# Four steps of a graph network moved to GpSimd, quarter tiles in its last layer, and a new planned order

## The chip, the cores and the metric

The kernel runs on one core of a Trainium2 chip. The metric is the device time of one execution in microseconds (us). Before the change it is 2740.81 us, the median of 3 runs (2739.89 to 2741.58).

## The reference

A stack of four graph layers on 16 independent graphs of 1024 nodes with 256 features; each layer takes `relu(layernorm(x))` and adds its result to x.

```python
# layer 0
h = h_in @ W_msg                                  # messages
msg = einsum('bij,biu->bju', adj, h) / deg        # sum over neighbours
x += relu(h_in @ W_upd + msg + bias)
# layers 1 and 2: attention with 4 heads of 64 (slope 0.01 and 0.2)
e = leaky_relu(e_src[i] + e_dst[j], slope)        # where adj, else -1e9
x += epilogue(softmax(e) @ h)   # 1: bias, relu, + h, layernorm per head; 2: elu
# layer 3: the same with one head of 256, slope 0.2, no epilogue
```

adj holds zeros and ones, is symmetric and has ones on its diagonal; some 3% of its entries are ones. All is float32.

## The kernel before

`tile_factored` does the work; `tile_general` is a second way that runs only if a check at the end (sums of adj, sizes of the exponents, denominators) is not met. With s and d the source and target terms, exp(leaky_relu(s+d)) is exp(slope s) exp(d) times the larger of exp((1-slope) s) and exp(-(1-slope) d), and the first factor drops out of the softmax, so that one VectorE instruction gives 128 x 1024 weights: `masked` (L1077) takes the maximum of a broadcast row r, which holds exp((1-slope) s) of the 1024 sources, with a per-partition scalar tt = exp(-(1-slope) d), and multiplies by the 0/1 mask. These tiles are called masks or weights here; they are the stationary side of the products. exp(d) is multiplied into the other side (`weigh`, L1242, for layers 1 and 2; a ScalarE scaling, L1407, for layer 3).

Per graph:
- layer 0: `norm_t` (norm and transposition: statistics on VectorE L922 and L929, a power on GpSimd L934 and L935, normalisation on ScalarE L954, transposition on PE L967). Four pairs of projections (L984) of the messages; each pair is split into a high part in the PE's rounded float32 format (ScalarE L1112) and a low part: PE subtracts the high one in PSUM with a product by minus identity (L1119), ScalarE copies the rest (L1129). Eight gathers (L1143, L1146) sum both over the neighbours. Each gather's result is scaled by the inverse degree (GpSimd L1157 and L1158, ScalarE L1164). For each pair of node blocks, PE adds the bias as a product of two rows (L1173) to the update projection (L1182); VectorE adds both (L1194) and adds the relu to x (L1201).
- `mask_block` loads adj, squares it on ScalarE into bytes and transposes it by DMA into the mask.
- layers 1 and 2, `heads`: norm, eight projections (L984, copied by ScalarE at L1003), `terms` (L1009): exp of the source terms on ScalarE (L1024), transposed on PE (L1034), copied (L1038), stored to DRAM by SP (L1042) and broadcast back as r, one row per head (L1067); VectorE's reductions for the range check (L1050 to L1052); two exponentials of d (L1057, L1058); `weigh`. Then for each of four heads eight masks of 128 x 1024 and eight products (L1266, 16 matmuls each), and an epilogue: division (L1285, L1286), layer 1's bias, relu, norm (L1310 to L1369), layer 2's elu (ScalarE L1381, L1382, VectorE L1388). Results of heads 0 to 2 go to x by an accumulating DMA from GpSimd's queue (L1216), that of head 3 by VectorE (L1227).
- layer 3: eight masks of 128 x 256 for each of four pairs of target blocks (L1083 with 256 columns), products of two matmuls (L1420), division and sum (L1434, L1445), store.

The order of all engines is written out by a planner (`Plan`, L72). Each step is given with `do`: engine, an assumed cost, reads, writes and a due time: the PE time of the steps of its graph before it, plus `b * SHIFT` (L1472), plus a constant per stage and engine (`RANK`). `emit` then repeatedly takes, of all steps that are ready, the one that can start first, with the smallest due time among equals, and gives out its instructions in that sequence. So several graphs are interleaved; each engine works its queue strictly in that order. `BUFS` (L52) says how many buffers stand behind each name: six mask buffers `p`, four PSUM banks `mm`, two of `hn`. `gates` lets a graph begin once the second before it has reached layer 3.

In the planned order of the steady part, PE's transposition of the source terms of layer 1 (L1034) of a graph is followed by 12 matmuls of layer 3 of the second graph before it (L1420), and then by that layer's first product. VectorE's order there: last scaling, last layer-2 epilogue of the graph before, norm statistics for that graph's layer 3, and then the first masks of layer 1.

Of the kernel before, what the change touches and what calls it, by code (L numbers as in the profile page):

```python
# [26 lines left out]
SHIFT = 38.75  # L27

ENGINES = ("pe", "dve", "act", "pool", "sp")
RANK = {  # L30
    "load": (-255, -45, -146, -223, -161),
    "setup": (147, 44, -129, 45, 72),
    "norm0": (132, -159, -111, 18, -3),
    "split0": (-94, 119, -51, -165, -111),
    "mask": (77, 143, 41, 193, 218),
    "gather0": (241, -7, 71, 23, 10),
    "norm1": (-60, -62, -162, -146, -99),
    "project1": (20, 26, -5, 26, -6),
    "weights1": (-164, 7, -45, 57, -13),
    "heads1": (-192, -212, -213, -62, -111),  # L40
    "last1": (-26, -102, 9, -196, -80),
    "norm2": (-206, -157, 81, 6, -21),
    "project2": (79, -60, -360, 87, -40),
    "weights2": (94, -3, 153, -153, 12),
    "heads2": (-112, -33, -288, -105, -59),
    "last2": (-21, -230, -230, -36, -82),
    "norm3": (-477, -373, -518, -355, -261),
    "project3": (148, 162, -14, -78, 0),
    "weights3": (170, 143, 167, 44, 87),
    "last3": (43, -259, -75, -14, -59),  # L50
# [4 lines left out]
    "mv": 4, "st": 2, "rstd": 4, "shift": 4, "tt": 3, "es": 2, "dg": 2, "rden": 2, "sth": 1, "mh": 2, "rsh": 2,  # L55
    "acc": 2, "mm": 4,
    "f_w0": 1, "f_w1": 1, "f_w2": 1, "f_w3": 1, "f_bias0": 1, "f_rows1": 1,
# [14 lines left out]
class Plan:  # L72
# [8 lines left out]
    def __init__(self):  # L81
        self.ops, self.pos, self.gate, self.stage = [], 0.0, None, None

    def do(self, eng, cost, fn, r=(), w=(), lag=0.0, slack=0.0, kind="f", dma=0.0):
# [25 lines left out]
        self.ops.append((eng, cost, lag, fn, deps, bufs, self.pos + slack + RANK[self.stage][ENGINES.index(eng)], kind, dma))  # L110
# [3 lines left out]
    def emit(self):  # L114
# [7 lines left out]
        kept, moved = "f", 0.0  # L122
# [6 lines left out]
        while ready:  # L129
            best = None  # L130
            for k in ready:
                eng, cost, lag, fn, deps, bufs, prio, kind, dma = self.ops[k]
# [18 lines left out]
                if at is not None and (best is None or (at, prio, k) < best):  # L151
                    best = (at, prio, k)
# [446 lines left out]
def tile_factored(  # L599
# [75 lines left out]
    def kept(name, shape, dtype=F32):  # L675

        t = const.tile(shape, dtype, name=name)
        return Buf(name, lambda: t)


    w0 = kept("f_w0", [P, KC, 2 * D])
    w1c = kept("f_w1", [P, KC, WC])
# [868 lines left out]
```

## Time and profile before

| | us |
|---|---|
| median of 3 runs | 2740.81 |
| the profiled execution's own time | 2741.27 |
| its span in the profile | 2739.4 |
| PE busy | 2547.4 |
| VectorE (DVE) busy | 2357.3 |
| ScalarE (ACT) busy | 1143.5 |
| GpSimd (POOL) busy | 878.0 |

The mean granted PE clock is 0.972 of full. Two queues carry nearly all of the 293.58 MB that DMA moves. The costliest groups are the masks (L1083, 1536 instructions, 1473.3 us on VectorE) and the products of layers 1 and 2 (L1266, 1064.6 us on PE).

A row of groups reads: line, engine, operation, output<-inputs, shape, x count | busy us, mean ns of one | idle time of the engine just before them, and what ended most of it. A row of the timeline: start, duration, engine, line, operation, and in brackets the idle time before it with what ended it. PE records two matmuls for each float32 matmul of the text.

### The profile page before, as it was taken

Reading aid. Unit: us, or ns where it says so; the run is one execution under the profiler, and the core shown is the slowest. Engines: PE = TensorE matmul, PEld = TensorE weight load, DVE = VectorE, ACT = ScalarE, POOL = GpSimd, SP = SyncE. Lnnn points to the kernel's source line nnn. Section 1 sums busy time; section 2 is a strip of 40 time slices with the busy share of each in tenths; the row PEclk is TensorE's granted clock in tenths of the full one; section 3 lists DMA queues with packets and bytes.
Section 4 is the critical chain, followed back from the end, with each engine's and each line's share of the span. In section 5 each row is a group of like instructions: output and inputs, shape, how many; then the busy total and the mean of one; then the engine's idle time right before and its main releaser. Section 6 shows DMA issues by size and latency. Waiting matters only on the chain. (4 is left out here: it accounts for less than half of the span.)

```text
span 2739.4 us, 92386 instructions
## 1 busy us (share of the span) xinstructions
PE 2547.4 (93%) x40667; PEld 2285.7 (83%) x40667; DVE 2357.3 (86%) x4790; ACT 1143.5 (42%) x2753; POOL 878.0 (32%) x907
## 2 busy tenths in 40 slices
PE   7867999999999999999999999999999999999786
PEld 6767798888888888889888889888888988888775
DVE  2699689898988989899898989989898898989884
ACT  4431625344353444525344452534435353453222
POOL 3332234324252332424224251422425133241210
PEclk9989999999999999999999999999999999999998
DMA  8724547356472745547255563735546263562121
GB/s 194 171 44 84 113 87 165 82 128 117 99 143 53 159 91 129 105 91 163 60 144 97 118 125 71 163 75 133 112 107 134 63 158 81 130 118 66 33 52 29
DMA packets 397318, 293.58 MB, mean 107 GB/s; under 512 B 179301, under 2 KB 345706, under 8 KB 396906
## 3 DMA queue, kind: packets, MB, share of 16 engines
q0 software_dynamic: 232992, 92.29, 24.8%
q1 hardware_dynamic: 160752, 193.05, 24.4%
q8 instruction: 321, 5.26, 0.8%
q10 hardware_dynamic: 3162, 2.24, 0.3%
q14 instruction: 91, 0.75, 0.1%
HBM read 228.21 MB, written 17.37 MB: 90 GB/s over the span
## 5 line engine op out<-in xcount | busy, mean ns | idle before, releaser
L1083 DVE SCALAR_TENSOR_TENSOR p<-r,tt,mask 128x1024 f32<-128x1024 f32 (+1 forms) x1536 | 1473.3, 1010 | 109.2 <-PE acc L1266 40.8
L1266 PE MATMUL acc<-wide,p 128*64 128x65 f32 x32768 | 1064.6, 227 | 135.7 <-DVE p L1083 129.3
L1266 PEld LDWEIGHTS acc<-wide,p 128*64 128x64 f32 x32768 | 1017.2, 141 | 204.0 <-issue 99.0
L984 PE MATMUL mm<-f_w,ht 128*128 128x264 f32 (+2 forms) x2048 | 477.0, 387 | 1.4 <-ACT ht L973 1.3
L1420 PE MATMUL acc<-wide,p 128*128 128x257 f32 x2048 | 462.2, 382 | 10.1 <-DVE p L1083 9.9
L1420 PEld LDWEIGHTS acc<-wide,p 128*128 128x128 f32 x2048 | 386.1, 191 | 68.1 <-issue 11.1
L984 PEld LDWEIGHTS mm<-f_w,ht 128*128 128x128 f32 x2048 | 384.6, 192 | 61.2 <-ACT ht L973 3.0
L954 ACT ACTIVATE hn<-x,shift,rstd 128x256 f32<-128x256 f32 x512 | 269.1, 591 | 257.5 <-DVE shift L941 157.1
L1356 ACT ACTIVATE t<-t,mh,rsh 128x64 f32<-128x64 f32 x512 | 176.7, 428 | 198.2 <-DVE mh L1346 174.3
L1143 PE MATMUL mm<-wide,adjr 128*128 128x258 f32 x1024 | 254.5, 289 | 0.0
L1146 PE MATMUL mm<-wide,adjr 128*128 128x256 f32 x1024 | 247.9, 282 | 0.0
L1003 ACT COPY wide<-mm 128x264 f32<-128x264 f32 (+1 forms) x384 | 141.3, 378 | 218.7 <-PE mm L984 216.5
L1216 POOL DMA_DIRECT2D x<-y x48 | 76.6, 1596 | 447.4 <-DVE y L1388 435.8
L934 POOL TENSOR_SCALAR rstd<-mv 128x4 f32<-128x4 f32 x128 | 60.7, 474 | 434.6 <-DVE mv L929 402.3
L1143 PEld LDWEIGHTS mm<-wide,adjr 128*128 128x128 f32 x1024 | 195.9, 191 | 1.7
L1146 PEld LDWEIGHTS mm<-wide,adjr 128*128 128x128 f32 x1024 | 194.2, 190 | 1.5
L922 DVE BATCH_NORM_STATS2 st<-x 128x6 f32<-128x256 f32 x512 | 183.2, 412 | 8.4 <-DMA x<-in_x_dram 5.6
L967 PE MATMUL mm<-f_ident,hn 128*128 128x128 f32 x1024 | 168.0, 300 | 20.2 <-ACT hn L954 17.2
L973 ACT COPY ht<-mm 128x512 f32<-128x512 f32 x256 | 137.8, 580 | 104.9 <-PE mm L967 103.9
L1157 POOL TENSOR_SCALAR dg<-f_deg 128x1 f32<-128x1 f32 x128 | 61.0, 476 | 359.7 <-ACT f_deg L1154 357.4
L967 PEld LDWEIGHTS mm<-f_ident,hn 128*128 128x128 f32 x1024 | 125.2, 151 | 50.4 <-ACT hn L954 35.5
L935 POOL TENSOR_TENSOR rstd<-rstd,f_mhalf 128x4 f32<-128x4 f32 x128 | 162.2, 1268 | 10.7
(103 smaller groups left out, 2179.3 us busy)
## 6 DMA issues: line engine op xcount, KB each, us to landing
r<-rd SPq DMA_DIRECT2D x144, 512.0 KB, 3.9
adjr<-in_adj_dram POOLq DMA_DIRECT2D x128, 512.0 KB, 4.7
nat<-in_adj_dram SPq DMA_DIRECT2D x128, 512.0 KB, 6.6
out_dram<-o SPq DMA_DIRECT2D x64, 256.0 KB, 2.8
x<-in_x_dram SPq DMA_DIRECT2D x31, 512.0 KB, 5.1
x<-t POOLq DMA_DIRECT2D x48, 256.0 KB, 5.5
x<-y POOLq DMA_DIRECT2D x48, 256.0 KB, 4.5
mask<-sq SPq DMA_TRANSPOSE x128, 4.7
```

What stands on the lines that cost most here:

```text
L922: lambda st=st, ib=ib, k=k: nc.vector.bn_stats(st.t[:, k, :], xs.t[:, ib, :]),
L935: nc.gpsimd.tensor_tensor(rstd.t, rstd.t, mhalf[:, :nh], op=ALU.pow)
L954: nc.scalar.activation(hn.t[:, k, :], xs.t[:, hf * nh + q, :], AF.Relu, bias=shift.t[:, q : q + 1], scale=rstd.t[:, q : q + 1],)
L967: nc.tensor.transpose(pt.t[:, k, c, :], hn.t[:, k, c * P : (c + 1) * P], ident)
L984: nc.tensor.matmul(out, ht.t[:, c, ib * P : (ib + 1) * P], w.t[:, c, lo:hi], start=(c == 0 and k == 0), stop=(c == KC - 1), skip_group_che ...
L1003: lambda ib=ib, ps=ps: nc.scalar.copy(wh.t[:, ib, :cols], ps.t[:, :cols]),
L1083: lambda: nc.vector.scalar_tensor_tensor(w.t[:, : hi - lo], r.t[:, lo:hi], tt.t[:, jb, h : h + 1], mask.t[:, jb, lo:hi], op0=ALU.max, op1= ...
L1143: nc.tensor.matmul(ps.t[:, : D + 2], a.t[:, ib, :], hi.t[:, ib, : D + 2], start=(ib == 0), stop=False)
L1146: nc.tensor.matmul(ps.t[:, :D], a.t[:, ib, :], lo.t[:, ib, :D], start=False, stop=(ib == NB - 1))
L1266: nc.tensor.matmul(ps.t[c : c + 64, g, q * E1 : (q + 1) * E1], p.t[:, i2 * 64 : (i2 + 1) * 64], xw.t[:, jb, h * E1 : (h + 1) * E1], start= ...
L1356: nc.scalar.activation(t.t[:, ib, :], t.t[:, ib, :], AF.Identity, bias=mb.t[:, 3, ib : ib + 1], scale=rs.t[:, ib : ib + 1],)
L1420: nc.tensor.matmul(ps.t[:, q, : D + 1], w.t[:, q * P : (q + 1) * P], wh.t[:, jb, : D + 1], start=(jb == 0), stop=(jb == NB - 1),)
```

## The change

- Low part of the messages: ScalarE copies the projection from PSUM to SBUF (into one of the two `hn` buffers) and GpSimd subtracts the high part (64 instructions of 128 x 512). PE's product by minus identity is gone.
- Layer 0's bias is loaded once to all partitions and added by GpSimd to the scaled sums (64 of 128 x 512); PE's bias product is gone, and so is the preparation of its two rows.
- Range check: GpSimd adds exponentials up over all layers and graphs (two additions of at most 64 columns in each of 48 layers), and one comparison at the end takes the largest sums; VectorE's three reductions per layer are gone.
- Scaling by exp(d) (`weigh`) goes from VectorE to GpSimd, 64 of 128 x 1024, with the small copies of layer 1.
- Layer 3: four masks of 256 columns share one `p` buffer.
- The planner: other costs, ranks and start offsets per graph (`START`), a tolerance within which a step of smaller due time goes first (`HOLD`), masks kept in one sequence per graph (`row`), and masks preferred when few are in stock (`LOW`, `FIRST`). The source terms' copy gets a buffer of its own (`r4`).

In the order that results, the transposition of layer 1's source terms is, for graphs 2 to 14, followed on PE at once by the first product of that layer. On VectorE the sequence at that place is the last layer-2 epilogue, the norm statistics of layer 3, and the first mask. At the start, graph 0 passes through layers 1 and 2 before graph 1's first product of layer 1.

```diff
-SHIFT = 38.75
+SHIFT = 101.5
+
+LOW, FIRST = 1, 28
 
 ENGINES = ("pe", "dve", "act", "pool", "sp")
+HOLD = (0.0, 0.05, 0.6, 0.0, 0.0)
+
+START = (232, 385, 200, 255, 176, 24, -46, -173, -79, -112, -264, -136, -283, -240, -391, -668)
...
-    "weights1": (-164, 7, -45, 57, -13),
+    "weights1": (-173, -73, -356, -76, 0),
...
-    "mv": 4, "st": 2, "rstd": 4, "shift": 4, "tt": 3, "es": 2, "dg": 2, "rden": 2, "sth": 1, "mh": 2, "rsh": 2,
+    "mv": 4, "st": 2, "rstd": 4, "shift": 4, "et": 3, "r4": 1, "dg": 2, "rden": 2, "sth": 1, "mh": 2, "rsh": 2,
...
+        if row is not None:
+            if row in self.rows:
+                deps.add(self.rows[row])
+            self.rows[row] = k
...
+                if stock > 0 and store < LOW:
+                    prio -= FIRST
...
+            until = at + HOLD[ENGINES.index(self.ops[k][0])]
+            for a, p, q in could:
+                if self.ops[q][0] == self.ops[k][0] and a <= until and p < prio:
+                    at, prio, k = a, p, q
+            eng, cost, lag, fn, deps, bufs, _, kind, dma, stock = self.ops[k]
+            store += stock
...
+        fetch(b0, "in", lambda t: t, bias0.rearrange("(o d) -> o d", o=1).to_broadcast([P, D]))
...
+        def raise_t():
+            nc.scalar.activation(et.t[:, 1], ed().rearrange("p n h -> p h n"), AF.Exp, scale=-(1.0 - slope))
+            nc.scalar.activation(ed(), ed(), AF.Exp)
+
+        do("act", 0.5, raise_t, w=[(et, 1), wh])
+
         def bounds():
-            es = wh.t[:, :, scol : scol + nh]
-            nc.vector.tensor_reduce(mx[:, k : k + 1], ed(), AX.XY, ALU.max)
-            nc.vector.tensor_reduce(mx[:, k + 1 : k + 2], ed(), AX.XY, ALU.min, negate=True)
-            nc.vector.tensor_reduce(mx[:, k + 2 : k + 3], es, AX.XY, ALU.max)
-
-        do("dve", 0.4, bounds, r=[wh])
-
-        def raise_t():
-            nc.scalar.activation(tt.t, ed(), AF.Exp, scale=-(1.0 - slope))
-            nc.scalar.activation(ed(), ed(), AF.Exp)
-
-        do("act", 0.5, raise_t, w=[tt, wh])
+            so_far = top
+            nc.gpsimd.tensor_tensor(
+                so_far[:, :2, :m], so_far[:, :2, :m], et.t.rearrange("p s h n -> p s (h n)"), op=ALU.add
+            )
+            v = so_far[:, 2, :m].rearrange("p (n h) -> p n h", h=nh)
+            nc.gpsimd.tensor_tensor(v, v, ed(), op=ALU.add)
+
+        do("pool", 0.9, bounds, r=[et, wh], w=[most], slack=5.143)
...
+    def masked(r, tt, mask, jb, h, lo, hi, w=None, q=0):
+
+
+        w = w or buf(work, "p", [P, N])
+        c = q * (hi - lo)
         do(
             "dve",
             (hi - lo + 125) / 960.0,
             lambda: nc.vector.scalar_tensor_tensor(
-                w.t[:, : hi - lo], r.t[:, lo:hi], tt.t[:, jb, h : h + 1], mask.t[:, jb, lo:hi], op0=ALU.max, op1=ALU.mult
+                w.t[:, c : c + hi - lo],
+                r.t[:, lo:hi],
+                tt.t[:, 1, h, jb : jb + 1],
+                mask.t[:, jb, lo:hi],
+                op0=ALU.max,
+                op1=ALU.mult,
             ),
-            r=[r, tt, mask],
-            w=[w],
+            r=[r, (tt, 1), mask],
+            w=[(w, q)],
+            row="weights",
+            stock=1,
...
-            do(
-                "pe",
-                0.23,
-                lambda n=n, ps=ps: nc.tensor.matmul(
-                    ps.t, minus, hi.t[:, n : n + 2, :D], start=False, stop=True, skip_group_check=True
-                ),
-                r=[(hi, ib) for ib in parts],
-                w=[ps],
-                kind="r",
-            )
+            raw = buf(work, "hn", [P, 2, D])
             do(
                 "act",
                 0.48,
-                lambda n=n, ps=ps: nc.scalar.copy(lo.t[:, n : n + 2, :D], ps.t),
+                lambda raw=raw, ps=ps: nc.scalar.copy(raw.t, ps.t),
                 r=[ps],
+                w=[raw],
+            )
+            do(
+                "pool",
+                1.3,
+                lambda n=n, raw=raw: nc.gpsimd.tensor_tensor(
+                    lo.t[:, n : n + 2, :D],
+                    raw.t,
+                    hi.t[:, n : n + 2, :D].bitcast(F32),
+                    op=ALU.subtract,
+                ),
+                r=[raw, *((hi, ib) for ib in parts)],
                 w=[(lo, ib) for ib in parts],
             )
...
-                nc.tensor.matmul(
-                    pu.t,
-                    pair.to_broadcast([2, P]),
-                    b0.t.rearrange("k (o d) -> k o d", o=1).to_broadcast([2, 2, D]),
-                    start=True,
-                    stop=False,
...
-            do("pe", 2.17, update, r=[(ht, jb // 2), (dg, "in"), w0, b0], w=[pu], kind="rf")
+            do("pe", 1.78, update, r=[(ht, jb // 2), (dg, "in"), w0], w=[pu])
+            do(
+                "pool",
+                1.3,
+                lambda o=o: nc.gpsimd.tensor_tensor(
+                    o.t, o.t, b0.t.rearrange("p (o d) -> p o d", o=1).to_broadcast([P, 2, D]), op=ALU.add
+                ),
+                r=[b0],
+                w=[o],
...
-            nc.vector.tensor_tensor(xwv[:, s, :, :E], whv[:, s, :, :E], ex.to_broadcast([P, 4, H, E]), op=ALU.mult)
+            nc.gpsimd.tensor_tensor(xwv[:, s, :, :E], whv[:, s, :, :E], ex.to_broadcast([P, 4, H, E]), op=ALU.mult)
             if keep:
-                nc.vector.tensor_copy(xwv[:, s, :, E:E1], ex)
+                nc.gpsimd.tensor_copy(xwv[:, s, :, E:E1], ex)
 
         for g in range(2):
-            do("dve", 1.2 if keep else 1.14, lambda g=g: weigh(g), r=[wh] if keep else [], w=[(xw, ("w", g))] if keep else [wh])
+            do("pool", 2.7 if keep else 2.5, lambda g=g: weigh(g), r=[wh] if keep else [], w=[(xw, ("w", g))] if keep else [wh])
...
-                w = masked(r, tt, mask, jb, 0, i2 * 2 * P, (i2 + 1) * 2 * P)
-
-                def product(w=w, ps=ps, jb=jb):
-                    for q in range(2):
+                q = jb % 4
+                w = masked(r, tt, mask, jb, 0, i2 * 2 * P, (i2 + 1) * 2 * P, w if q else None, q)
+
+                def product(w=w, ps=ps, jb=jb, q=q):
+                    for k in range(2):
+                        c = (2 * q + k) * P
                         nc.tensor.matmul(
-                            ps.t[:, q, : D + 1],
-                            w.t[:, q * P : (q + 1) * P],
+                            ps.t[:, k, : D + 1],
+                            w.t[:, c : c + P],
                             wh.t[:, jb, : D + 1],
                             start=(jb == 0),
                             stop=(jb == NB - 1),
                         )
 
-                do("pe", 0.87, product, r=[w, (wh, jb)], w=[ps])
+                do("pe", 0.875, product, r=[(w, q), (wh, jb)], w=[ps], stock=-1)
...
```

## The prediction

> **What bounds the kernel now.** I read the head of the page first: one engine is near full, a second is not far behind.
>
> ```profile
> span 2739.4 us, 92386 instructions
> ...
> PE 2547.4 (93%) x40667; PEld 2285.7 (83%) x40667; DVE 2357.3 (86%) x4790; ACT 1143.5 (42%) x2753; POOL 878.0 (32%) x907
> ```
>
> These are averages over stages, so the next view cuts the span (columns: stretch, length, busy time of PE, weight loads, VectorE, ScalarE and GpSimd with instruction counts, granted clock, DMA share, GB/s):
>
> ```profile
> 100.00:300.00 200.00, 150.64 (x3272) 136.38 (x3271) 186.29 (x351) 60.06 (x147) 60.01 (x47) 0.90 0.41 82
> ...
> 1200.00:1362.00 162.00, 156.44 (x2565) 140.78 (x2561) 147.06 (x299) 71.81 (x175) 55.56 (x56) 0.99 0.52 113
> 1362.00:1524.00 162.00, 155.92 (x2505) 140.23 (x2500) 145.11 (x297) 69.87 (x170) 55.54 (x56) 0.98 0.52 113
> ...
> 2500.00:2740.00 240.00, 190.16 (x2938) 167.85 (x2934) 179.23 (x356) 58.05 (x142) 32.73 (x28) 0.90 0.20 43
> ```
>
> 162 us is one graph's period in the steady part: the same instruction (exp of the source terms of layer 1) starts at 402.5 us for graph 2 and at 2349.4 us for graph 14, 12 graphs later. There PE is busy for 156 of 162 us and VectorE for 146. Only at the two ends (100 to 300 us and after 2500) does VectorE set the pace. So the steady part, some 14 of 16 graphs, is worth what happens to PE's time. What stops PE there? Its waits between 300 and 2500 us (us in total, times, longest):
>
> ```profile
> PE acc L1266 <- DVE p L1083: 60.2, 26, 4.1
> ```
>
> Nearly all of this is one gap per graph: 13 gaps of 3.9 to 4.1 us, one of 3.4 for graph 2, each between an L1420 product and the first L1266 product of the next graph. One of them in order of time:
>
> ```profile
> 1220.04 0.28 PE L1034 MATMUL mm<-f_ident,es 128*32 128x128 f32 x1
> 1220.16 5.37 PE L1420 MATMUL acc<-wide,p 128*128 128x257 f32 x24
> 1229.66 1.74 PE L1266 MATMUL acc<-wide,p 128*64 128x65 f32 x32 [4.13 <-DVE p L1083]
> ```
>
> and VectorE in the same microseconds:
>
> ```profile
> 1220.16 0.21 DVE L1285 RECIPROCAL rden<-acc 128x8 f32<-128x8 f32 x1
> 1220.40 0.69 DVE L1286 TENSOR_TENSOR t<-acc,rden 128x512 f32<-128x512 f32 x1
> 1221.01 1.66 DVE L1083 SCALAR_TENSOR_TENSOR p<-r,tt,mask 128x256 f32<-128x256 f32 x4
> 1222.59 0.68 DVE L1388 SCALAR_TENSOR_TENSOR y<-y,t 128x512 f32<-128x512 f32 x1
> 1223.31 0.69 DVE L1227 TENSOR_TENSOR x<-x,y 128x512 f32<-128x512 f32 x1
> 1224.03 1.40 DVE L922 BATCH_NORM_STATS2 st<-x 128x6 f32<-128x256 f32 x4
> ...
> 1228.23 2.47 DVE L1083 SCALAR_TENSOR_TENSOR p<-r,tt,mask 128x1024 f32<-128x1024 f32 x2
> ```
>
> Graph k's last layer-2 product ends at 1220.1. VectorE normalises it, ScalarE takes its ELU, VectorE adds it to x and takes the statistics of layer 3's norm; only then, in its written order, comes the first layer-1 mask of graph k+1. PE bridges the first 5.4 us with layer-3 products (L1420, 24 records = 12 matmuls of the text) kept back for it, then stands 4.13 us.
>
> **The change part by part.**
>
> *PE work removed: the minus and bias products.*
>
> ```profile
> L1173 PE MATMUL mm<-f_bias,f_pair 2*128 2x512 f32 x64 | 31.6, 494 | 0.0
> L1119 PE MATMUL mm<-wide,f_minus 128*128 128x512 f32 x64 | 24.2, 451 | 0.7 <-ACT wide L1112 0.7
> ```
>
> 31.6 + 24.2 = 55.8 us, 3.5 per graph; by spacing of starts (a bias product at 55.26, the next matmul at 55.69: 0.43; a minus product at 53.03, the next at 53.26: 0.23) it is 64 x 0.66 = 42, 2.6 per graph. I take 3.0 per graph; 14 steady graphs give -42 us (ends -36 and -49).
>
> *VectorE work removed:* the scaling (L1247 76.6 us, L1249 5.6) and the range check's reductions (L1050 to L1052: 26.2), 108 us or 6.8 per graph. In the steady part that is beside PE and buys nothing by itself. At the two ends it is on the path: about 5 scalings before graph 2's first mask and 2 after 2500 us, some 2.4 us each, -17 us, against which stands the next item.
>
> *GpSimd work added:* 64 subtractions and 64 bias additions of 128x512, 64 scalings of 128x1024, and 128 small ones. No row has a large GpSimd tensor operation. The Trainium skill's "GPSIMD Engine Reference", section 3.1, gives 4497 ns for a two-input addition of 2048 columns, 2.2 ns each: estimates of 1.1 us for 512 and 2.25 for 1024. Per graph 4 x 1.1 + 4 x 1.1 + 4 x 2.25 + about 1 = 19 us beside the 55.5 it has: GpSimd stays under half full. What speaks against the change is where it reads. In the trace a tiny GpSimd operation waits out a VectorE mask:
>
> ```profile
> 1404.15 1.09 POOL L934 TENSOR_SCALAR rstd<-mv 128x4 f32<-128x4 f32 x1 [10.78 <-DVE mv L929]
> ...
> 1406.91 0.23 POOL L934 TENSOR_SCALAR rstd<-mv 128x4 f32<-128x4 f32 x1 [0.55 <-DVE shift L941]
> ```
>
> The first overlaps a mask, the second runs while VectorE is idle: 1.09 against 0.23. The reverse, VectorE held by GpSimd, can't show with reads of 4 columns. The skill's "SBUF — State Buffer", section "Who interferes with whom", says it is symmetrical: a VectorE instruction with two SBUF inputs and a GpSimd instruction that reads SBUF exclude each other for the whole instruction. The masks, L1369, L1318, L1310, L1201, L1388 and L1227 have two, 69% of the time between 300 and 2500. By the rule VectorE loses 19 x 0.69 = 13 us per graph and nets 146 - 6.8 + 13 = 152; by the row alone it loses nothing and nets 139. Both are below PE's 153, so most of it is hidden; what is not is local: while the subtractions of graph k+1 run, masks come at half rate, and only six mask buffers stand between them and PE. I take 0.7 us per graph (+10 us), ends 0 and 4 (0 and +55). At the ends of the run the same loss (5 + 2 scalings of two halves, 4.5 x 0.69 = 3.1 us each, 22) eats the 17 saved: 0 together.
>
> *Waits the move adds.* Subtraction: gather waits for its four lo pairs; the order leaves 7 to 10 products (6.7 to 9.6 us) between the last layer-0 projection and the first gather, against about 1.2 us of ScalarE copies plus at worst 2.3 per subtraction, most of them already begun: hidden. Bias: it stands in GpSimd's queue between the inverse degree and VectorE's add, with the adjacency loads, pow and accumulating stores behind it; the sums are due 7 us later: hidden. Scaling: two halves after ACT's exp, done before the chain below ends. If these covers failed each would cost 1 to 3 us a graph; that is inside the 0-to-4 above.
>
> *Quarter tiles and the new order.* Layer-3 masks now fill one 1024-column buffer by four, so VectorE can run 24 ahead instead of 6; its waits for L1420 (24.9 us in the steady part) are VectorE's, and worth nothing to PE. The written-out order matters more. I followed each layer's transposition of the source terms in PE's order and summed what stands behind it before the first product that needs it. Before, for layer 1 of graphs 3 to 15: 12 layer-3 matmuls, 5.4 us (the L1420 row above). After, for graphs 2 to 14: nothing at all; the transposition is followed at once by the first product, and graph 15 has 1 us. The layer-3 products that bridged the gap stand earlier (behind layer 2's transposition, which has 15 to 17 us in both). VectorE's order has the same sequence as before: reciprocal, t, y, x, statistics of both halves, and then the first mask. So the bridge goes, and only the work that VectorE did for it (four quarter-width masks under the ELU, and 1.0 us of layer-3 outputs at 1227.2) leaves the chain. From the rows above: last product ends 1220.1; second statistics end at 1227.2 without the outputs; one mask of 1.2 us; 0.2 to PE as now: first product at 1228.5, a gap of 8.4 us instead of 4.13. Through the other branch (transposition, ScalarE copy at 1220.36, store at 1220.64, row broadcasts issued at 1222.07, median 3.9 us to landing) the mask could start at 1226.0, so VectorE's chain decides. 14 graphs x 4.3 = +60 us; ends 6.0 (the ELU chain partly overlapped) and 9.5 (y and the x addition, both with two SBUF inputs, behind a scaling on GpSimd), +27 and +75.
>
> *The start* is ordered anew too: graph 0 goes through layers 1 and 2 alone. At its change of layer both engines follow one chain (the last head's epilogue, norm, projection, row broadcast), some 20 us by the rows (3 on VectorE, 2.5 on GpSimd, 2.7 on ScalarE, 4 more on VectorE, then the norm and 6 us of broadcast). Against it PE has 72 instead of 83 us of work ahead of the first product (-11), and the 11.0 us that layer-3 masks of graph 0 wait for their row near 314 us are covered (37 us of PE work stand between, before 10). I take 0, ends -15 and +20.
>
> Clock: PE's grant falls to half for 3.4 to 6.8 us once per graph after this gap; one gap per graph remains, so I add nothing.
>
> **Sum**, against the profiled execution's span: 2739.4 - 42 + 10 + 60 = 2767; that execution took 2741.3 against a median of 2740.8, so no correction: **2767 us**, +1.0%.
>
> **Rivals.** (1) *PE's relief decides: faster.* The steady part is full of PE, and 42 to 56 us of PE work go. The one place on which it turns is the gap: from 4.1 + 42/14 = 7.1 us downward the change wins. If ScalarE's ELU and the x addition come early enough for a gap of 6.0, and VectorE loses nothing: 2739.4 - 49 + 27 - 15 at the ends = 2702. For it: VectorE gets 6.8 us a graph, and the wait for ScalarE ahead of L1050 (72.3 us in the steady part) leaves its queue. Against it: the gap is a chain of dependent rows, not a lack of VectorE time. (2) *VectorE becomes the bound.* If the exclusion holds for all 19 us and the masks it delays aren't caught up, the period is 139 + 19 + the chain's 8 = 166 or more: 2739.4 + 14 x 4.5 + 10 = about 2812. For it: 1.09 against 0.23; against it, that GpSimd's share meets masks only in part. (3) *They cancel:* a gap of 7.1 us without loss, 2741.
>
> **Chances.** Forecast 0.50 (2748 to 2795); VectorE bound 0.16 (2795 to 2840); cancelled 0.10; faster 0.24. Under about 0.2% (5.5 us) a measurement of this kernel can't tell a change from none. So slower 0.66, same 0.10, faster 0.24. The range leaves out the lower part of rival 1 and the upper of rival 2: 2700 to 2815; the forecast's own is 2748 to 2795, and as cases of both signs are in the wide one, it stands beside it.
>
> **What would show it.** Right: one PE gap of 8 to 9 us per graph ahead of the first layer-1 product, released by the mask, with VectorE's y, x and statistics in it; a period of about 164; PE busy near 2495. The bias and minus rows gone. Exclusion right: masks that start late beside a GpSimd tensor operation, and subtractions above 2 us where a mask runs. Wrong: a gap below 7 us, or masks so late that PE waits through the layers.

## The result and the profile after

The changed kernel takes 2914.68 us (median of 4 runs, 2908.73 to 2919.69) against 2740.35 us of the kernel before on the same chip: a ratio of 1.064, 95% interval [1.061, 1.066]. It is slower by 174 us. I had forecast 2767 us, slower by 26, with a range that ended at 2815.

The head of the page of the changed kernel, and two stretches of its steady part (columns as before: stretch, length, busy time of PE, weight loads, VectorE, ScalarE and GpSimd, granted clock, DMA share, GB/s):

```profile
span 2910.9 us, 92029 instructions
...
PE 2535.7 (87%) x40539; PEld 2300.7 (79%) x40539; DVE 2394.9 (82%) x4548; ACT 1145.5 (39%) x2753; POOL 1244.8 (43%) x1228
```

```profile
1200.00:1362.00 162.00, 140.98 (x2433) 128.58 (x2432) 134.98 (x242) 64.26 (x151) 62.14 (x62) 0.93 0.49 98
1362.00:1524.00 162.00, 144.43 (x2263) 131.42 (x2262) 137.74 (x256) 66.21 (x160) 76.15 (x70) 0.96 0.47 95
```

No engine is full. PE is busy for 141 to 144 of 162 us where it had 156; VectorE, from which 108 us of work were taken, is busy for 38 us more over the run; and the granted clock is 0.93 to 0.96 where it had 0.99 and 0.98. What stops PE between 300 and 2600 us (the view of its waits: total, times, longest) is, besides the one gap per graph, a number of small waits for masks, and a wait for layer 2's norm that hardly existed before:

```profile
PE acc L1289 <- DVE shift L948: 122.1, 13, 10.4
PE acc L1289 <- DVE p L1093: 80.2, 74, 3.4
PE mm L974 <- ACT hn L961: 31.8, 13, 3.5
```

All of the loss lies in the steady part. Layer 1's first product of graph 2 starts at 419.6 us before and at 416.0 after, that of graph 15 at 2527.9 and 2707.0, and from there to the end it is 211 and 204 us. So the new order of the start gains 4 us and the end 8, and the 13 graphs between lose 183.

The gap that I had followed is there, in PE's and VectorE's order of time:

```profile
1283.45 0.28 PE L1040 MATMUL mm<-f_ident,et 128*32 128x128 f32 x1
1293.90 3.74 PE L1289 MATMUL acc<-wide,p 128*64 128x65 f32 x64 [10.17 <-DVE shift L948]
```

```profile
1283.57 0.21 DVE L1308 RECIPROCAL rden<-acc 128x8 f32<-128x8 f32 x1 [3.92 <-PE acc L1289]
...
1285.86 0.69 DVE L1411 SCALAR_TENSOR_TENSOR y<-y,t 128x512 f32<-128x512 f32 x1 [1.36 <-ACT y L1405]
...
1290.20 0.36 DVE L936 BATCH_NORM_AGGREGATE mv<-st 128x2 f32<-128x6 f32 x4
1292.47 1.28 DVE L1093 SCALAR_TENSOR_TENSOR p<-r,et,mask 128x1024 f32<-128x1024 f32 x1 [1.91 <-DMA r<-rd]
```

The view puts PE's wait down to L948, a small operation between the first two masks; the product reads the first mask, which ended at 1293.75. 13 such gaps sum to 122 us, 9.4 each (forecast 8.4, before 4.13).

What I had sized far too small is in the next lines, VectorE and GpSimd in the same microseconds:

```profile
806.71 1.28 DVE L1093 SCALAR_TENSOR_TENSOR p<-r,et,mask 128x1024 f32<-128x1024 f32 x1
807.90 1.25 DVE L1369 SCALAR_TENSOR_TENSOR mh<-mh,rsh 128x8 f32<-128x8 f32 x1
809.08 5.79 DVE L1093 SCALAR_TENSOR_TENSOR p<-r,et,mask 128x1024 f32<-128x1024 f32 x3
```

```profile
806.92 5.66 POOL L1144 TENSOR_TENSOR wide<-hn,wide 128x512 fp32r<-128x512 f32 x3
```

Alone a subtraction takes 1.26 us (the shortest of the 64), a bias 1.25, a scaling 1.88. Here, one by one in the trace, the three masks take 2.37, 2.30 and 1.27 us, where a mask alone takes 1.28, and the three subtractions 2.21, 1.27 and 2.26: the two engines take turns. A VectorE operation on eight columns takes 1.25 us in place of 0.16.

Two sums over the whole trace are used below. "Lengthened" is the time by which VectorE's instructions exceed the median of their line and shape, where that is more than 0.05 us: 0 before, 138 us after, of it 63 with a subtraction beside them, 55 with a bias, 10 with a scaling. VectorE is busy for 94% of the subtractions' time and 86% of the bias's, but for 22% of the scaling's. The second is PE's time per graph, from each matmul's start to the next one's, over ten graphs of the steady part; a pause of over 0.8 us counts as a wait of the matmul that ends it.

| us per graph | minus and bias | products of layers 1, 2 | waits ahead of them | transpositions with their waits | the rest | period |
|---|---|---|---|---|---|---|
| before | 2.84 | 64.42 | 4.71 | 9.90 | 80.4 | 162.3 |
| after | 0 | 67.22 | 15.72 | 11.39 | 81.8 | 176.1 |
| e1, no reads | 0 | 65.27 | 11.33 | 8.64 | 80.8 | 166.0 |
| e3, bridge back | 0 | 68.33 | 10.54 | 11.39 | 81.7 | 172.0 |
| e9, both | 0 | 66.36 | 7.27 | 8.50 | 80.6 | 162.8 |
| e10, two on VectorE | 0 | 65.98 | 12.31 | 9.64 | 81.1 | 169.0 |

### The profile page after: what moved, and what is told of

Its sections match the earlier page's. It is cut to its first block, busy times and chain, and to the rows that moved or that the text cites. A ratio compares the mean times of both kernels' runs of the same rounds, so it can differ in the third digit from the quotient of the medians.

```text
span 2910.9 us, 92029 instructions
## 1 busy us (share of the span) xinstructions
PE 2535.7 (87%) x40539; PEld 2300.7 (79%) x40539; DVE 2394.9 (82%) x4548; ACT 1145.5 (39%) x2753; POOL 1244.8 (43%) x1228
## 3 DMA queue, kind: packets, MB, share of 16 engines
q0 software_dynamic: 232960, 92.29, 27.2%
q10 hardware_dynamic: 3304, 2.37, 0.3%
## 5 line engine op out<-in xcount | busy, mean ns | idle before, releaser
L1093 DVE SCALAR_TENSOR_TENSOR p<-r,et,mask 128x1024 f32<-128x1024 f32 (+1 forms) x1536 | 1545.2, 1064 | 123.7 <-DMA r<-rd 57.2
L1289 PE MATMUL acc<-wide,p 128*64 128x65 f32 x32768 | 1089.7, 229 | 282.7 <-DVE p L1093 136.8
L1289 PEld LDWEIGHTS acc<-wide,p 128*64 128x64 f32 x32768 | 1041.3, 144 | 348.8 <-DVE p L1093 156.0
L1445 PEld LDWEIGHTS acc<-wide,p 128*128 128x128 f32 x2048 | 392.0, 193 | 66.8 <-issue 8.7
L1163 PE MATMUL mm<-wide,adjr 128*128 128x258 f32 x1024 | 261.9, 295 | 6.8 <-ACT o L1184 3.8
L941 POOL TENSOR_SCALAR rstd<-mv 128x4 f32<-128x4 f32 x128 | 74.9, 585 | 403.1 <-DVE mv L936 379.3
L1163 PEld LDWEIGHTS mm<-wide,adjr 128*128 128x128 f32 x1024 | 200.2, 195 | 10.6 <-ACT o L1184 4.3
L1166 PEld LDWEIGHTS mm<-wide,adjr 128*128 128x128 f32 x1024 | 198.5, 194 | 0.7
L1404 ACT ACTIVATE y<-t 128x512 f32<-128x512 f32 x64 | 40.4, 632 | 387.0 <-DVE t L1309 387.0
L942 POOL TENSOR_TENSOR rstd<-rstd,f_mhalf 128x4 f32<-128x4 f32 x128 | 154.5, 1207 | 10.7
```

Source lines behind the costliest of these rows:

```text
L942: nc.gpsimd.tensor_tensor(rstd.t, rstd.t, mhalf[:, :nh], op=ALU.pow)
L1093: lambda: nc.vector.scalar_tensor_tensor(w.t[:, c : c + hi - lo], r.t[:, lo:hi], tt.t[:, 1, h, jb : jb + 1], mask.t[:, jb, lo:hi], op0=ALU ...
L1163: nc.tensor.matmul(ps.t[:, : D + 2], a.t[:, ib, :], hi.t[:, ib, : D + 2], start=(ib == 0), stop=False)
L1166: nc.tensor.matmul(ps.t[:, :D], a.t[:, ib, :], lo.t[:, ib, :D], start=False, stop=(ib == NB - 1))
L1289: nc.tensor.matmul(ps.t[c : c + 64, g, q * E1 : (q + 1) * E1], p.t[:, i2 * 64 : (i2 + 1) * 64], xw.t[:, jb, h * E1 : (h + 1) * E1], start= ...
L1445: nc.tensor.matmul(ps.t[:, k, : D + 1], w.t[:, c : c + P], wh.t[:, jb, : D + 1], start=(jb == 0), stop=(jb == NB - 1),)
```

## The experiments

The planner writes one list of all operations; the runs that edit the order move entries of that list once it is planned, and leave everything else where the planner put it. The diffs are shortened to the calls that change, each on one line. Each ratio is to the kernel before, with its 95% interval.

**e1, the changed kernel without GpSimd's reads.**

```diff
-lambda n=n, raw=raw: nc.gpsimd.tensor_tensor(lo.t[:, n : n + 2, :D], raw.t, hi.t[:, n : n + 2, :D].bitcast(F32), op=ALU.subtract),
+lambda n=n, raw=raw: (nc.gpsimd.tensor_copy(lo.t[:, n : n + 2, :1], raw.t[:, :, :1]), nc.gpsimd.memset(lo.t[:, n : n + 2, :D].bitcast(F32), 0.0)),
-lambda o=o: nc.gpsimd.tensor_tensor(o.t, o.t, b0.t.rearrange("p (o d) -> p o d", o=1).to_broadcast([P, 2, D]), op=ALU.add),
+lambda o=o: nc.gpsimd.memset(o.t, 0.1),
-nc.gpsimd.tensor_tensor(xwv[:, s, :, :E], whv[:, s, :, :E], ex.to_broadcast([P, 4, H, E]), op=ALU.mult)
+nc.gpsimd.memset(xwv[:, s, :, :E], 0.37)
```

> The changed kernel with its written order untouched, in which GpSimd's large new operations (low half's subtraction, bias, scaling) are replaced by memsets of the same width, which write and read nothing; so the low half, the bias and the scaling are left out of the computation. Exclusion theory (GpSimd's reads hold VectorE, 131 us of VectorE time lengthened in the trace, and PE waits for it): VectorE's lengthened masks go and the time falls by most of that, to 2770-2810 us. Order theory (the loss is the written order: no layer-3 products kept back ahead of layer 1, and VectorE queued behind a layer-3 reciprocal): masks become even, but the time stays at 2880-2910 us, with the gap of 9 us ahead of layer 1 and the wait of 5-12 us at the reciprocal still there.

2765.85 us, ratio 1.010 [1.007, 1.012]: 149 us less than the changed kernel. VectorE's rows, after and then without the reads (count | busy us, mean ns | idle before):

```profile
L1093 DVE SCALAR_TENSOR_TENSOR p<-r,et,mask 128x1024 f32<-128x1024 f32 x1024 | 1328.1, 1349 | 119.6 <-PE acc L1289 54.5 <-DMA r<-rd 53.1 <-PE acc L1445 11.8
```

```profile
L1093 DVE SCALAR_TENSOR_TENSOR p<-r,et,mask 128x1024 f32<-128x1024 f32 x1024 | 1254.2, 1276 | 107.3 <-PE acc L1289 50.3 <-DMA r<-rd 41.8 <-PE acc L1445 12.0
```

Lengthened time falls from 138 to 2 us, VectorE's busy time by 137, and the end comes 149 us earlier. The gap ahead of layer 1 stays (11.33 us of waits in the table). One thing else changes: a memset of 512 columns takes 0.53 us and one of 1024 takes 0.95, so GpSimd's queue is shorter too. Little of that reaches VectorE: its waits that a GpSimd operation ended (the view of its waits over the whole run) go from 42 us in the changed kernel to 35. The runs e5 and e6 bear on it as well.

**e2, the moves in the old order.** The kernel before with its list, in which only the steps change engine:

```diff
-ps.t, minus, hi.t[:, n : n + 2, :D], start=False, stop=True, skip_group_check=True
-nc.scalar.copy(lo.t[:, n : n + 2, :D], ps.t)
+nc.scalar.copy(raw.t, ps.t)
+nc.gpsimd.tensor_tensor(lo.t[:, n : n + 2, :D], raw.t, hi.t[:, n : n + 2, :D].bitcast(F32), op=ALU.subtract)
-pair.to_broadcast([2, P]),
+nc.gpsimd.tensor_tensor(o.t, o.t, bb.rearrange("p (o d) -> p o d", o=1).to_broadcast([P, 2, D]), op=ALU.add)
-nc.vector.tensor_tensor(xwv[:, s, :, :E], whv[:, s, :, :E], ex.to_broadcast([P, 4, H, E]), op=ALU.mult)
+nc.gpsimd.tensor_tensor(xwv[:, s, :, :E], whv[:, s, :, :E], ex.to_broadcast([P, 4, H, E]), op=ALU.mult)
```

> The kernel before with its own written order, in which only the moves are made: the low half by a ScalarE copy and a GpSimd subtraction, the bias by GpSimd, the scaling by GpSimd, each at the place of what it replaces; full tiles for layer 3, the range check as before. Order theory: the PE relief of 42 us arrives and the exclusion costs the 10 us that I forecast: 2700-2720 us. Exclusion theory: the moves alone cost what the changed kernel lost beyond the gap, 2800-2860 us. Masks of 128x1024 longer than 2 us should show beside GpSimd's operations in either case, about 60 of 1024.

2862.86 us, ratio 1.045 [1.043, 1.048]. With the bridge in place and full tiles, the moves alone cost 124 us. VectorE's operations are lengthened by 167 us (69 beside the scaling, 43 and 42 beside the subtraction and the bias, 13 beside loads).

**e8, the same without reads** (memsets as in e1, so low half, bias and scaling are left out):

> The second run (the moves in the order of before) with GpSimd's large new operations as memsets of the same width, so low half, bias and scaling are left out. Measures the other terms of my sum without the exclusion: PE loses its 128 products, VectorE its scaling. Forecast by the sum: 2740 - 42 = 2698 us (2680-2705), as no bridge is lost. Rival: waits for the moved steps (gather ahead of the subtraction, layer 1's first product) keep it at 2740 or more.

2766.51 us, ratio 1.009 [1.008, 1.011]. The reads were worth 96 us here, but the kernel isn't faster than before, though PE lost its 128 products. PE's waits show what took their place:

```profile
PE mm L1146 <- POOL wide L1559: 35.0, 14, 2.7
```

The gather, which follows closely in the old order, waits 2.6 us per graph for low halves that stand in GpSimd's queue behind an accumulating store of layer 1, and its matmuls take 2.0 us more per graph. (46 us of the gathers' time fall where the granted clock is at half, against 3 before.) The rival held.

**e3, the bridge back.** In the changed kernel's list, for graphs 2 to 14:

```diff
+order = place(order, masks[:4], last, before=True)
+order = place(order, masks[4:], last)
+order = place(order, products, turn)
+order = place(order, ends, first, before=True)
```

Here masks and products are the last eight of layer 3 of the graph two back, last is the final normalisation of layer 2, turn layer 1's transposition, and ends the outputs of that group, put ahead of the first mask of layer 1.

> The changed kernel, in whose written order one thing is edited for graphs 2 to 14: the last 8 layer-3 products of the graph two back (one output group) stand behind layer 1's transposition again, with four of their masks ahead of and four behind the last normalisation of layer 2. Order theory: the gap ahead of layer 1's first product falls from 9.4 us to 2-4, worth 5-7 us a graph: 2820-2850 us. Exclusion theory: the gap closes, but the masks that are late afterwards take the time back: 2885-2915 us.

2859.5 us, ratio 1.044 [1.042, 1.046]: 55 us less than the changed kernel. The gap falls to 2.8 us (35.9 us in 13). Neither theory is enough alone: the bridge is worth nearly what I gave it, and two thirds of the loss stay.

**e4, the reciprocal later.** In the changed kernel VectorE stands 12 us at a layer-3 reciprocal, having run ahead with quarters:

```profile
1213.57 3.25 DVE L1093 SCALAR_TENSOR_TENSOR p<-r,et,mask 128x256 f32<-128x256 f32 x8
1228.83 0.17 DVE L1459 RECIPROCAL f_rdn<-acc 128x2 f32<-128x2 f32 x1 [12.01 <-PE acc L1445]
```

```diff
+order = place(order, ends[3 * i : 3 * i + 3] + stores[i : i + 1], masks[n - 1])
```

> The changed kernel, in whose written order one thing is edited: the first layer-3 reciprocal (with its two outputs) behind the last of a graph's layer-3 masks moves behind the next three full masks of layer 2, so that VectorE doesn't stand at it with those masks queued. Order theory: three masks of 1.2 us go into the wait of 5-12 us, 3.6 us of VectorE time a graph, and PE's waits of layer 2 fall by as much: 2860-2890 us. Rival: layer 2's masks can't start there anyway because the mask buffers are full of layer-3 quarters that PE hasn't taken, and the wait moves from the reciprocal to the mask: 2905-2920 us.

2914.04 us, ratio 1.062 [1.059, 1.065], no change. Between 300 and 2600 us the wait at the reciprocal falls from 132.3 us to 13.5, and this line of VectorE's waits rises from 27.2 to:

```profile
DVE p L1093 <- DMA r<-rd: 153.0, 25, 13.3
```

The masks that stood behind the reciprocal had no row yet. The wait was real and cost nothing; the rival's number held, but it is the row broadcast and not the mask buffers that stops them.

**e5, e6 and e7, the disputed cost by itself.** The kernel before, with its list, and unused work at the 128 places of the subtraction and the bias:

```diff
+*(nc.gpsimd.tensor_tensor(dd, lo.t[:, n + j, :D].bitcast(F32), dd, op=ALU.subtract) for j in range(2))
+[nc.gpsimd.tensor_tensor(dd, dd, dd, op=ALU.subtract) for j in range(2)]
```

in e6 with nc.gpsimd.memset(dd, 0.0) and a copy of one column in their place, and in e7 with nc.vector.tensor_tensor(dd, dd, dd, op=ALU.subtract) at both.

> The kernel before with all its work in its order, plus work that nobody uses: at each of the 128 places where the change puts a subtraction or a bias, GpSimd does two extra subtractions of 128x256 on SBUF (the four low halves or a scratch tile read, a scratch tile written). VectorE-time theory (what GpSimd's reads take from VectorE reaches the end almost in full, whatever VectorE's idle share): VectorE's operations are lengthened by 90-130 us in all and the time rises by 80-130, to 2820-2870 us. Rival (VectorE has room; the second run's loss came from consumers waiting for the moved work, the gather for the subtraction and layer 1 for the scaling): VectorE's operations lengthen as much, but the time stays at 2740-2770 us.

> The twin of the run with unused reads: the same places, with memsets of 128x256 on GpSimd in place of the subtractions (and one column copied to keep the place). Both theories: 2735-2750 us, as VectorE's operations keep their length. If it rises by as much as its twin, the cause is GpSimd's queue (late inverse degrees, loads and stores), not the reads.

> The same unused subtractions (two of 128x256 at 128 places) on VectorE itself, in the kernel before: about 128 x 0.8 = 100 us more VectorE work, nothing on GpSimd. VectorE-time theory: the time rises by 70-110 us, to 2810-2850: VectorE's idle 14 in 100 can't take it. Rival (VectorE's slack takes it, as I forecast for the added 6 us a graph): 2740-2765 us.

e5: 2854.77 us, ratio 1.041 [1.040, 1.043]. e6: 2763.96 us, ratio 1.008 [1.007, 1.010]. e7: 2807.73 us, ratio 1.024 [1.022, 1.026]. Masks in e5, and in its twin e6:

```profile
L1083 DVE SCALAR_TENSOR_TENSOR p<-r,tt,mask 128x1024 f32<-128x1024 f32 x1024 | 1286.8, 1311 | 46.4 <-PE acc L1266 39.6 <-PE acc L1420 5.0 <-DMA r<-rd 1.9
```

```profile
L1083 DVE SCALAR_TENSOR_TENSOR p<-r,tt,mask 128x1024 f32<-128x1024 f32 x1024 | 1251.5, 1278 | 51.2 <-PE acc L1266 44.6 <-PE acc L1420 5.0 <-DMA r<-rd 1.1
```

So reading costs 91 us more than writing, with 69 us of lengthened time (less than the 90 to 130 that I gave), although nobody reads what GpSimd computes. The memsets are also shorter than the subtractions (0.31 us against 1.09 and 0.90 on average), so this pair doesn't keep GpSimd's queue equal. What a later queue does shows in VectorE's wait for layer 1's power, over the whole run in the kernel before, in e6 and in e5:

```profile
DVE mh L1346 <- POOL rsh L1340: 17.4, 49, 0.4
```

```profile
DVE mh L1346 <- POOL rsh L1340: 33.1, 49, 1.6
```

```profile
DVE mh L1346 <- POOL rsh L1340: 48.5, 49, 1.6
```

The 23 us of e6 come without any lengthening, and 16 us more of this wait come with them; of the 91 us between e5 and e6 the wait has 15, against 69 of lengthening. And e7 shows that VectorE's time matters: 95 us more VectorE work, with no GpSimd in it, cost 67 us in a kernel whose VectorE idles for 14% of the span.

**e9, bridge back and no reads**, the edits of e1 and e3 together:

> The changed kernel with both edits of runs 1 and 3: the 8 layer-3 products kept back ahead of layer 1, and memsets in place of GpSimd's large new operations (low half, bias and scaling left out). If lost bridge and exclusion are two separate terms: 2766 - 55 = 2711 us (2700-2725), which is the 2740 of before less PE's 40. If the exclusion's loss had only taken the place of the gap's (one hides the other), the second edit brings much less: 2740-2766 us.

2725.36 us, ratio 0.994 [0.992, 0.995]. The two terms are largely separate (40 us for the bridge without the reads, 55 with them). Against the kernel before, 14 us are gained where PE's work fell by 40, although this run also has the quarter tiles (e11); it computes less and is no kernel to use.

**e10, two of the steps on VectorE**, scaling left with GpSimd:

```diff
-nc.gpsimd.tensor_tensor(lo.t[:, n : n + 2, :D], raw.t, hi.t[:, n : n + 2, :D].bitcast(F32), op=ALU.subtract)
+nc.vector.tensor_tensor(lo.t[:, n : n + 2, :D], raw.t, hi.t[:, n : n + 2, :D].bitcast(F32), op=ALU.subtract)
-nc.gpsimd.tensor_tensor(o.t, o.t, b0.t.rearrange("p (o d) -> p o d", o=1).to_broadcast([P, 2, D]), op=ALU.add)
+nc.vector.tensor_tensor(o.t, o.t, b0.t.rearrange("p (o d) -> p o d", o=1).to_broadcast([P, 2, D]), op=ALU.add)
```

> The changed kernel, its written order untouched, with the low half's subtraction and the bias on VectorE at their places; only the scaling and the range check's sums stay with GpSimd. In the changed kernel's trace VectorE's operations are lengthened by 63 us beside the subtractions and 55 beside the bias; on VectorE the two cost about 128 x 0.68 = 87 us. If what VectorE loses decides: 118 - 87 = 31 us less VectorE time, and GpSimd's queue shorter: 2870-2900 us. Rival: an operation of 0.68 us in VectorE's queue, which waits there for ScalarE's copies, costs more than the same on GpSimd: 2920-2960 us.

2825.88 us, ratio 1.032 [1.030, 1.033]: 89 us less than the changed kernel, three times what I expected. VectorE's own row for the subtraction:

```profile
L1144 DVE TENSOR_TENSOR wide<-hn,wide 128x512 fp32r<-128x512 f32 x64 | 43.9, 686 | 7.8 <-ACT hn L1137 7.8
```

Lengthened time falls by 125 us, VectorE's busy time by 50. To do the two steps on VectorE is cheaper for VectorE than to let GpSimd do them.

**e11, whole tiles for layer 3**: a buffer for each layer-3 mask in place of one for four (VectorE's masks move back where six buffers don't suffice).

```diff
-w.t[:, c : c + hi - lo],
+w.sub[q].t[:, c : c + hi - lo],
-w.t[:, c : c + P],
+w.sub[q].t[:, c : c + P],
```

> The changed kernel with a mask buffer for every layer-3 mask as before, in place of one for four; PE, ScalarE, GpSimd and SyncE keep their order, and VectorE's masks move back only where six buffers don't suffice. If running 24 masks ahead is worth nothing to PE, as I forecast: 2890-2930 us. If the quarters do feed PE (its layer-3 products would wait for masks otherwise): 2950-3000 us. If they are harmful (VectorE spends 10 us on masks that PE takes late): below 2890 us.

2950.61 us, ratio 1.076 [1.073, 1.079]. The quarters gain 36 us in the changed order. I had given them nothing.

**e12, PE relief that costs neither VectorE nor GpSimd**: in the kernel before, ScalarE writes the bias into the accumulator.

```diff
-pair.to_broadcast([2, P]),
+nc.scalar.copy(pu.t, b0.t.rearrange("p (o d) -> p o d", o=1).to_broadcast([P, 2, D]))
-start=False, stop=(q == 1 and c == KC - 1),
+start=False, stop=(c == KC - 1), skip_group_check=True,
```

> The kernel before with one PE relief that costs neither VectorE nor GpSimd anything: ScalarE writes layer 0's bias into the accumulator of the update two PE steps ahead of it, and PE's 64 bias products go; everything else, the minus products and all orders, as before. If PE's relief is worth its time when no other engine pays for it: 1.7 us a graph in the steady part, -24 us, 2712-2725 us. Rival: the update now waits for ScalarE, whose queue has copies and activations of other layers ahead of it: 2735-2770 us.

2754.39 us, ratio 1.006 [1.004, 1.007]. PE's 1.70 us per graph are gone, and these came: 1.6 us per graph of waiting for the write, which stood behind a copy that waits for GpSimd's pow, and 0.5 more for layer 2's norm.

```profile
PE mm L1182 <- ACT mm L1565: 20.9, 13, 1.6
PE mm L967 <- ACT hn L954: 12.6, 13, 1.0
```

**e13, e14, e15 and e17, the gap of the kernel before.** All in the kernel before, with four layer-3 masks to a buffer; e13 keeps eight products back instead of six, e14 also puts two masks of layer 1 between the halves of layer 3's statistics, e15 is e14 with the bias written by ScalarE, earlier in its queue than in e12, and e17 is e13 with layer 3's last outputs behind the third mask. The lines stand in this order, one for each step:

```diff
+order = place(order, products, turn)
+order = place(order, masks, half)
+order = fills(plan, order)
+order = place(order, ends, masks[2])
```

> The kernel before (all steps on their engines) with layer 3's masks four to a buffer and, for graphs 3 to 15, eight layer-3 products kept back behind layer 1's transposition in place of six. If a microsecond of this gap is worth a microsecond of time: the gap falls from 4.13 us by two products of 0.87 to 2.4 us, 13 x 1.7 = 22 us, and a little of the half clock behind it: 2705-2722 us. Rival: the gap's time returns as masks that are late elsewhere: 2735-2745 us.

> As the run with eight products kept back, and VectorE's first two masks of layer 1 placed between the two halves of layer 3's statistics, where their row broadcast has just landed. If the gap is worth its length: the first product comes at 1.2 us after the landing, the gap shrinks to about 0.5 us: 13 x 3.6 = 47 us, and half of the half-clock time of 85 us: 2670-2695 us. Rival: layer 3's norm is 2.4 us later and its transpositions now stop PE: 2700-2720 us.

> As the run with early masks, and layer 0's bias written into the accumulator by ScalarE, ahead of the copies that it stood behind in the run with the bias on ScalarE alone, so that PE's bias products go. If PE's relief arrives where PE doesn't wait for the write: another 13 x 1.7 = 22 us. Rival: PE is no longer what sets the period, VectorE's masks are: no change, within 5 us of the run without it.

> As the run with eight products kept back, and layer 3's last reciprocal and two outputs (1.0 us on VectorE) behind the first three masks of layer 1 in place of ahead of them; layer 3's norm keeps its place. If the gap is worth its length and nothing waits for the outputs: 13 us less than with eight products alone, 2720-2728 us. Rival: VectorE has the same work to do and the next masks are late by it: 2733-2740 us, no change from that run.

e13: 2736.32 us, ratio 0.9985 [0.998, 0.999]; e14: 2766.41, ratio 1.009 [1.007, 1.010]; e15: 2777.77, ratio 1.014 [1.013, 1.016]; e17: 2748.2, ratio 1.002 [1.002, 1.003]. None got what the length of the gap promised, and three were worse than their rival's number. In e13 most gaps fall from 4.13 to 2.5 to 3.0 us, and yet PE's waits for layer 1's and 2's masks between 300 and 2500 us stay at 59.3 us in 41 pieces, against 60.2 in 26: they come later. In e14 these waits fall to 2.2 per graph, and layer 3's norm, delayed by 2.4 us, stops PE instead:

```profile
PE mm L967 <- ACT hn L954: 48.0, 26, 3.3
```

In e15 the same wait is 65.2 us.

e13 is ahead by less than the 0.2% that I named as the limit of telling; no run gave a version that computes everything and clearly beats the kernel before.

**e16, the scaling alone** on GpSimd, in the kernel before:

```diff
-nc.vector.tensor_tensor(xwv[:, s, :, :E], whv[:, s, :, :E], ex.to_broadcast([P, 4, H, E]), op=ALU.mult)
+nc.gpsimd.tensor_tensor(xwv[:, s, :, :E], whv[:, s, :, :E], ex.to_broadcast([P, 4, H, E]), op=ALU.mult)
```

> The kernel before with the scaling alone on GpSimd, in its place in the written order; VectorE loses 82 us of work. By run 2's trace its reads lengthen VectorE's operations by 69 us, so VectorE's time stays about even: 2735-2755 us. If the time follows where the masks are held (between the scaling and layer 1's and 2's first products, where PE has only six masks ahead): 2760-2790 us. If VectorE's 82 us count: below 2720 us.

2747.24 us, ratio 1.0025 [1.002, 1.003]. VectorE gives away 82 us of work and gets 67 us of lengthened masks: an even trade, as expected. By difference from e2, and if the steps simply add up, the loss in the old order is that of the subtraction and the bias, about 117 us with their waits.

## Why the prediction was wrong

*The direction and the gap were right.* The order leaves nothing behind layer 1's transposition; I gave that 60 us, and putting it back is worth 55 (e3). The gap is 9.4 us and not 8.4: in all 13 gaps the first mask waits for the row broadcast, for 0.1 to 2.1 us (1.9 in the row above, 1.1 on average), the branch that I had let VectorE's chain win.

*The step that failed is "+10 us" for exclusion.* I worked out by the rule of the Trainium skill ("SBUF — State Buffer", section "Who interferes with whom") that VectorE loses 13 us per graph, and then took 0.7, because VectorE's 152 us would be below PE's 153 and "most of it is hidden". The trace agrees with the rule in kind, as the two engines take turns, and roughly in size: VectorE is lengthened by 138 us over 16 graphs, 8.6 per graph, and GpSimd's three new steps by 56 us, 3.5 per graph (their busy time less 64 of the shortest of each). The sign that I had named for it, subtractions above 2 us, is in the rows (2.21 and 2.26), and so is the sign of being wrong, masks so late that PE waits through the layers (80.2 us in 74 waits beside the gap). The share of 69% that I used is an average; beside the subtraction and the bias VectorE is busy for 94% and 86% of the time. The discount was wrong. e1 puts the price at 149 us, e5 against e6 at 91 for unused work in the places of two of the three steps. An engine at 86% with waits of its own in every graph has no slack to sell: PE is only six masks behind it, and e7 shows 0.7 us of time for each us of VectorE work. The cover of "1 to 3 us a graph", "inside the 0-to-4", had the same flaw, as its upper end was also set by a comparison of averages.

With 149 in place of 10 my own sum is 2739.4 - 42 + 149 + 60 = 2906, 5 us from the span of 2910.9. That it comes so close is in part luck: the other two terms were both too large (e9 leaves 14 of the 42, and without the reads the bridge is worth 40), and with opposite signs.

*That the clock adds nothing* was wrong too. The grant is at half for 154 us in all before and for 325 after; PE is busy in 116 and 204 us of these. If PE works at half rate there, which is an estimate from the grant, that is 58 and 102 us lost: 44 more. It is about what keeps PE's busy time at 2536 where I had written 2495. The stretches at half go from 28 to 51 while PE's pauses multiply; without the reads they are 33, and PE is busy in 136 us of them, so most of this lies inside e1's 149.

What a microsecond of VectorE is worth isn't one number: 0.7 us of time in e7, 1.1 in e1 (149 for 137), 1.3 between e5 and e6 (91 for 69), 1.8 in e10 (89 for 50). By the same estimate the half clock has 34 us of e1's difference, 24 of that between e5 and e6 and 41 of e10's, but 12 of e7's. So part of what lengthened masks cost beyond plain work is the clock; where the rest comes from stays open.

*The -42 us for the bias and minus products* measured 2.84 us per graph as PE's work, against my 3.0, and so was sized right. But a microsecond taken from PE isn't a microsecond of time: it came to +26 us in e8, +15 in e12 and -14 in e9, which has the quarter tiles and the new order besides. In e8 and e12 the traces show what came back, PE's waits for the engine that got the step; for e9 no run divides the 14. In the changed order the gather didn't wait for the subtraction, as forecast (its time per graph rose by 0.3 us).

*That quarter tiles are worth nothing to PE* was wrong by 36 us (e11), in the change's favour. The long wait that running ahead makes at the reciprocal is free (e4).

*Rival 2* (VectorE becomes the bound, 2812) had the right mechanism and too small a price: it added up VectorE's busy time, the exclusion and the chain to a period of 166 us, while the period became 176 with VectorE busy for 135 to 138 of 162 us. Here no engine is full, and VectorE's delays set the pace all the same.

## What to carry to other kernels

When two engines feed each other through a few buffers in a written order, the less busy one need not have free time in proportion to its idle share: add a microsecond to it somewhere and see, before you call a cost hidden. A step moved to GpSimd that reads SBUF can cost VectorE more than the step itself, here 0.98 and 0.86 us per subtraction and bias of 128x512 against 0.69 on VectorE; it costs little where VectorE stands idle anyway, as beside most scalings of the changed order (10 us of lengthening with VectorE busy for 22% of their time, 67 in the old order with 81%). And a step taken from the full engine must leave no wait behind: look at who gets it and what stands ahead of it in that queue.

## What the runs showed of the hardware that I had not expected

- GpSimd's two-input operations are faster than I estimated for 1024 columns and slower for 512: 1.88 and 1.25 us when undisturbed, against 2.25 and 1.1. Memsets of these widths take 0.95 and 0.53 us and lengthen nearly nothing (2 us in all in e1; 0 in e6, with 256 columns).
- The lengthening also hits tiny operations: eight columns on VectorE take 1.24 to 1.78 us beside a subtraction or a bias in place of 0.16 (L1369, 17 of 64, 22 us in all), and GpSimd's sums of 64 columns for the range check take up to 1.35 us in place of 0.32 (L1062).
- GpSimd's pow reads SBUF too and lengthens nothing: the 64 on eight columns take 2.35 us each in the kernel before (L1340), 120 of their 150 us lie beside VectorE's operations with two SBUF inputs, and VectorE's lengthened time there is 0.
